# Four PSUM banks as one lasting tile, and attention's clips and exponentials on two banks at a time, in a two-layer cross-attention and feed-forward kernel

## The chip, the cores and the metric

The kernel runs on 1 core of one Trainium2 chip. The metric is device time in microseconds (us) of one execution. Engines are named as the profile names them: PE is TensorE's matmul pipe and PEld its weight loads, DVE is VectorE, ACT is ScalarE, POOL is GpSimd, SP issues most of the DMAs. PSUM is the memory that matmuls write; a tile of 128 partitions by 512 float32 values is called a bank here, and no matmul of this kernel writes across two.

## The reference

Eight batches of 112 tokens (512 wide) go through two layers, each a cross-attention and a feed-forward, with a layer norm in front of each and the result added to `x`. The context has 375 rows per batch.

```python
x = x + _L0_xattn_ref(_layernorm(x), ctx_2048, mask_bool)     # one head, keys and values are ctx itself
x = x + _L0_ffn_ref(_layernorm(x), w1, w2, w3)                # bit-linear: ternary weights, 8-bit activations
x = x + _L1_xattn_ref(_layernorm(x), ctx_2048, mask_int, Wq, bq, Wk, bk, Wv, bv, Wo, bo, ...)
x = x + _L1_ffn_ref(_layernorm(x), wq_gate, s_gate, wq_up, s_up, wq_down, s_down)
```

The change lies in the third line, and it touches the fourth through the PSUM banks. The third line's attention has 16 heads of 32:

```python
scores = einsum('bhsd,bhtd->bhst', q, k) / sqrt(32)
scores = clip(scores, -50, 50)
scores = clip(where(attend, scores, -10000.0), -50, 50)
probs  = softmax(scores)
ctx    = einsum('bhst,bhtd->bhsd', probs, v)
delta  = layernorm(clip(residual_scale, 0, 0.3) * (ctx @ Wo.T + bo)) * ln_gamma + ln_beta
```

The fourth line is `down(silu(gate(x)) * up(x))` with a hidden width of 1408 and integer weights minus 128, scaled per row.

## The kernel before

Line numbers are those of the kernel before, as the profile has them.

**Token layout.** The 8 x 112 tokens are 7 tiles of 128 (`tokens`, `xs`). Layer 1's matmuls over tokens go in two groups, tiles 0 to 3 (512 columns) and tiles 4 to 6 (384 columns) (`GROUPS`).

**Order.** PE's and SP's instructions run in the order in which the code writes them throughout. From layer 0's attention to its end, and in layer 1's attention, the order on DVE, ACT and POOL is also the written one; in the queries (L764 to L780) and in the last feed-forward those three engines are ordered by the scheduling layer. That layer also places every semaphore wait. It takes them from the tiles: a tile is what `pool.tile(...)` returns, an instruction that reads a tile waits for the one that wrote it, and one that writes it waits for those that read it before. A pool with `bufs=4` hands out four buffers in turn, and a new tile in a buffer waits until the old tile in the same buffer has been used up.

**PSUM from layer 1 on.** `ps_s` (L708) is a pool of four one-bank tiles, all called `s`; `ps_mm` (L709) has two, called `mm`; attention adds `num` and `den` (`ps_av`), and the last feed-forward adds two called `down` (`ps_d`).

**Who uses `ps_s`, in order:**

- `queries(g)` (L730 to L749): for each of four 128-row pieces `dc` of Wq, eight matmuls into an `mm` tile (L738, L740), then four into an `s` tile (L744); ACT moves `mm` to `qT` (L746), and DVE subtracts the `s` tile from it (L748). It runs for group 0, then for group 1.
- `transpose2(i)` (L222 to L236), for token tiles 4, 5 and 6 between the pieces of group 0's queries: four PE transposes into an `s` tile (L227), an ACT copy (L230), a DVE subtraction that reads the same `s` tile (L233), and a DVE operation on SBUF (L234).
- `scores(b, c)` (L899 to L912), for each of the 8 batches `b` and 3 context chunks `c` of 125: four `s` tiles, one for each 32-row strip `r` of the key and query projections; 16 matmuls of 32 x 125 weights and 112 columns (L905), with `dc` outside and `r` inside, so that four heads' scores fill each tile; then for each `r` a DVE clip from PSUM to an SBUF tile `e` (L910) and an ACT exponential in place (L911).
- `hits` (L992), one small matmul at attention's end, whose maximum decides between two ways of doing the last feed-forward; here the first, `feed_forward1`, is run.
- `gate_up1(g, ...)` (L1035 to L1055): for each of 11 pieces `hc` of the hidden width a gate tile and an up tile. It is called for pieces 0 and 1 of group 0, then `project(6)` runs, then for pieces 2 to 10, then after the down projections of group 0 for all 11 pieces of group 1.
- `transpose4` (L840) for token tiles 4, 5 and 6, between the down projections of group 0.

The core of `gate_up1`, one piece:

```python
gate = ps_s.tile([P, 512], F32, name="s")                                  # L1039
up = ps_s.tile([P, 512], F32, name="s")                                    # L1040
...                                                                        # 8 matmuls into gate, then 8 into up: L1045
nc.scalar.activation(gu, gate, AF.Silu, scale=sg)                          # L1050
nc.vector.scalar_tensor_tensor(gu, up, su, gu, ALU.mult, ALU.mult)         # L1051
nc.scalar.copy(gus[0], gu)                                                 # L1053
nc.vector.tensor_sub(gus[1], gu, gus[0])                                   # L1054
```

**Around the scores.** In each turn of attention's loop (L957 to L1002) PE also runs a step of the next batch's key and value projections (`fill`, L194 and L203), the sums of the chunk before (`sums`: L926 and L931) and, from batch 2 on, an output projection (L803) with its layer norm on DVE and POOL. `add(b)` (L893) adds the exponentials of chunk 1 to those of chunk 0, on POOL except for the last batch. `divide(b)` (L941) takes reciprocals (L947) and multiplies (L948) on DVE. `project_begin` and `project_end` (L806, L820) hold the layer norm's DVE and POOL operations (L809 to L828).

Of the kernel before, what the change touches and what calls it, by code (L numbers as in the profile page):

```python
# [23 lines left out]
F32 = mybir.dt.float32  # L24
# [6 lines left out]
ALU = mybir.AluOpType  # L31
AX = mybir.AxisListType
PSUM = bass.MemoryType.PSUM
ENGINES = mybir.EngineType

P = 128
B, T, D = 8, 112, 512
KC = D // P
S2, CK = 375, 125
NCK = S2 // CK  # L40
# [5 lines left out]
NR = P // HD  # L46
# [10 lines left out]
CLIP = 50.0 / SC1  # L57
# [7 lines left out]

SPLIT = 2.0 ** -12
LESS = 1.0 - 2.0 ** -13


@with_exitstack  # L70
def two_layers(ctx: ExitStack, tc: tile.TileContext, x, ctxT, ctxN, mask0, mask1, w1, w2, w3,
               wq, wk, wv, wo, bq, bk, bv, bo, gamma, beta, rscale,
               wg, sg, wu, su, wd, sd, out):
    nc = tc.nc
# [147 lines left out]
    def transpose2(i, psum):  # L222
# [6 lines left out]
        high, low, diff = (t[:, :, j * P:(j + 1) * P] for t in h2T[g])  # L229
        nc.scalar.activation(high, pt, AF.Identity, scale=LESS)  # L230

# [7 lines left out]
    with tc.tile_pool(name="w0", bufs=1, side="right") as w0p, \  # L239
# [290 lines left out]
        with tc.tile_pool(name="work1", bufs=2, side="right") as work1:  # L530
# [90 lines left out]
            for i in range(2, NT):  # L621
# [54 lines left out]
                elif i == 4:  # L676
# [3 lines left out]
                                                 for name in ("wq_high", "wq_low", "h2T_high"))  # L680
                    nc.scalar.activation(wq_high, wq_s, AF.Identity, scale=LESS)
                    nc.gpsimd.tensor_sub(wq_low, wq_s, wq_high.bitcast(F32))
# [22 lines left out]

    tailp = ctx.enter_context(tc.tile_pool(name="tailp", bufs=1, side="right"))

    ps_s = ctx.enter_context(tc.tile_pool(name="ps_s1", bufs=4, space=PSUM))  # L708
    ps_mm = ctx.enter_context(tc.tile_pool(name="ps_mm1", bufs=2, space=PSUM))  # L709
    kv_psum[0] = ps_mm  # L710

# [11 lines left out]
    upper = tailp.tile([CK, NCK, B], F32, name="upper")  # L723
# [127 lines left out]
    with tc.tile_pool(name="work2", bufs=1, side="right") as work2, \  # L851
# [21 lines left out]
        def convert_integers():  # L873
            for raw, which, half, c, n in loaded:
# [12 lines left out]

        sets = [[work2.tile([P, KC, T], F32, name=f"e{i}{r}") for r in range(NR)]  # L890
                for i in range(NCK)]

        def add(b):  # L893
            add = (nc.gpsimd if b in ADD_POOL else nc.vector).tensor_add
            for r in range(NR):
                e, e1 = (sets[(b + c) % NCK][r][:CK] for c in range(2))
                add(e, e, e1)  # L897

        def scores(b, c):  # L899
            kT = kvs_of[b][0]  # L900
            ss = [ps_s.tile([CK, KC, T], F32, name="s") for r in range(NR)]
            for dc in range(KC):
                for r in range(NR):
                    rows = slice(r * HD, (r + 1) * HD)
                    nc.tensor.matmul(ss[r][:, dc, :], lhsT=kT[rows, dc, c * CK:(c + 1) * CK],  # L905
                                     rhs=qT[rows, dc, b * T:(b + 1) * T], start=True, stop=True)
            es = sets[(b + c) % NCK]
            for r in range(NR):
                e = es[r][:CK]
                nc.vector.tensor_scalar(e, ss[r], upper[:, c, b:b + 1], -CLIP, ALU.min, ALU.max)  # L910
                nc.scalar.activation(e, e, AF.Exp, scale=SC1)  # L911
            return es  # L912

# [41 lines left out]
        for b in range(B):  # L957
            for c in range(NCK):
                if c == 2 and b in ADD_POOL:
                    add(b)  # L960
                if (b, c) in due:
                    convert_integers()
                    if counts:
                        load_integers(counts.pop(0))
                es = scores(b, c)
                if c == 2 and b not in ADD_POOL:
                    add(b)
# [237 lines left out]
```

## Time and profile before

| what | value |
|---|---|
| median of 3 runs | 517.08 us (516.91 to 518.55) |
| the profiled execution | 516.34 us, of which the span from the first to the last instruction is 514.2 us |
| granted PE clock, mean | 0.997 |
| queries, 213.20 to 235.30 us | PE busy 21.91 of 22.10 us |
| attention, 235.30 to 395.60 us | PE busy 158.84 of 160.30 us, DVE 124.70, ACT 98.28, POOL 83.48 |
| gate and up, group 0, with `project(6)`, 395.60 to 439.50 us | PE busy 43.90 of 43.90 us, DVE 25.70, ACT 13.90 |
| gate and up, group 1, 462.20 to 492.70 us | PE busy 30.50 of 30.50 us, DVE 13.15, ACT 11.55 |

How to read it: the busy time of an engine is the time covered by its instructions' rows. Matmuls overlap each other, and their ends are modelled, so PE's share near 100% says only that there is hardly a hole between matmuls. The profile's groups give, for one line and one shape, the count, the total busy time, the mean of one in ns, and how long the engine had stood idle in front of them and for whom. The chain of waits runs from the last instruction back to what released it, step by step.

### The profile page before, as it was taken

The page shows a single profiled execution, that of the slowest core. Times are in us where ns is not written, and L with a number is a line of the kernel's source. Part 1 is how long each engine was busy: PE and PEld are TensorE (multiplying, and loading weights), DVE is VectorE, ACT ScalarE, POOL GpSimd, SP SyncE. Part 2 cuts the span into 40 slices and gives each one's busy share as a digit, 9 for nine tenths or more (in the row PEclk, how much of TensorE's full clock was granted, in tenths as well). Part 3 has the DMA queues.
Part 4 walks back from the last instruction along what each step waited for, and adds up shares of the span by engine and source line. Part 5 has one row for each costly group of instructions (what it writes and reads, how often), then busy time and mean ns, then how long its engine had stood idle before and what let it go on. Part 6 is the DMA issues. An engine that isn't in the chain of part 4 may idle for free.

```text
span 514.2 us, 8868 instructions
## 1 busy us (share of the span) xinstructions
PE 502.5 (98%) x3402; PEld 315.8 (61%) x3402; DVE 337.2 (66%) x815; ACT 252.8 (49%) x438; POOL 134.4 (26%) x221
## 2 busy tenths in 40 slices
PE   9999999999999999999999999999999999999995
PEld 6445554455545455696565565555555788889984
DVE  3552548767798987965676688986897753334432
ACT  0326656857565666236675366465665233103310
POOL 0000121110111064211551475674754430000000
PEclk9999999999999999999999999999999999999998
DMA  8998795200120100122421112012320000010001
GB/s 241 347 407 326 268 324 205 80 18 0 61 82 1 60 2 0 45 101 61 162 68 51 62 52 62 3 53 62 98 69 13 20 1 1 20 42 20 1 20 48
DMA packets 13489, 45.77 MB, mean 89 GB/s; under 512 B 2097, under 2 KB 3392, under 8 KB 12288
## 3 DMA queue, kind: packets, MB, share of 16 engines
q1 hardware_dynamic: 11888, 41.43, 23.5%
q0 software_dynamic: 1248, 3.70, 2.2%
q8 instruction: 29, 0.48, 0.4%
q14 instruction: 20, 0.16, 0.1%
q10 hardware_dynamic: 304, 0.01, 0.0%
HBM read 41.46 MB, written 1.84 MB: 84 GB/s over the span
## 4 chain that ended last, share of the span: by engine, by line
PE 47%; DVE 6%; POOL 2%; ACT 1%; DMA 1%; issue 1%; DVEq 0%; POOLq 0%; ACTq 0%
PE s L1045 14%; PE mm L203 8%; PE down L1067 7%; PE mm L803 3%; PE s L905 3%; PE num L931 2%; PE mm L194 2%; DVE e L910 2%; PE den L926 2%; PE mm L740 1%; PE mm L738 1%; DMA raw<-in_wd_dram 1%; PE s L744 1%; DVE e L947 1%; ACT e L911 1%
## 5 line engine op out<-in xcount | busy, mean ns | idle before, releaser
L203 PE MATMUL mm<-wv,cT 128*125 128x512 f32 x192 | 87.6, 599 | 0.0
L194 PE MATMUL mm<-cT,wk 128*128 128x375 f32 x256 | 87.3, 485 | 0.0
L1045 PE MATMUL s<-h4T,w 128*128 128x512 f32 (+1 forms) x352 | 72.6, 367 | 0.2 <-PE num L931 0.2
L1045 PEld LDWEIGHTS s<-h4T,w 128*128 128x128 f32 x352 | 63.5, 188 | 8.8 <-PE num L931 0.4
L910 DVE TENSOR_SCALAR e<-s,upper 125x448 f32<-125x448 f32 x96 | 59.0, 677 | 14.7 <-PE s L905 13.9
L911 ACT ACTIVATE e<-e 125x448 f32<-125x448 f32 x96 | 51.6, 570 | 27.8 <-DVE e L910 27.3
L194 PEld LDWEIGHTS mm<-cT,wk 128*128 128x128 f32 x256 | 46.8, 190 | 27.6 <-issue 1.0
L203 PEld LDWEIGHTS mm<-wv,cT 128*125 128x125 f32 x192 | 34.5, 187 | 38.0 <-issue 36.4
L897 POOL TENSOR_TENSOR e<-e,e 125x448 f32<-125x448 f32 x28 | 33.1, 1213 | 15.8 <-PE num L931 15.8
L1067 PE MATMUL down<-w,gu 128*128 128x512 f32 (+1 forms) x176 | 37.0, 367 | 0.0
L541 PE MATMUL mm<-w_q,q_qT 128*128 128x512 fp8e4 (+1 forms) x168 | 34.8, 361 | 0.8 <-DVE tokens L583 0.4
L439 POOL DMA_DIRECT2D tokens<-x x14 | 10.7, 768 | 90.3 <-DVE x L433 63.0
L1067 PEld LDWEIGHTS down<-w,gu 128*128 128x128 f32 x176 | 29.8, 188 | 5.7
L880 ACT ACTIVATE w<-raw,zero_point 128x640 fp32r<-128x640 int32 (+2 forms) x29 | 22.6, 781 | 20.4 <-DMA raw<-in_wd_dram 9.2
L1053 ACT CAST gu<-gu 128x512 fp32r<-128x512 f32 (+1 forms) x22 | 12.5, 568 | 39.6 <-DVE gu L1051 39.6
L570 POOL TENSOR_SCALAR q<-gu 128x704 bf16<-128x704 f32 x14 | 10.8, 790 | 79.8 <-ACT gu L567 79.8
L882 POOL TENSOR_SCALAR w<-raw 128x640 fp32r<-128x640 int32 (+2 forms) x29 | 20.7, 724 | 36.0 <-ACT w L880 35.8
L905 PE MATMUL s<-qT,kv 32*125 32x112 f32 x768 | 29.4, 280 | 0.6 <-DVE qT L748 0.3
L1051 DVE SCALAR_TENSOR_TENSOR gu<-s,su,gu 128x512 f32<-128x512 f32 (+1 forms) x22 | 15.1, 684 | 21.8 <-PE s L1045 20.6
L905 PEld LDWEIGHTS s<-qT,kv 32*125 32x125 f32 x768 | 24.5, 183 | 7.1 <-issue 5.8
L541 PEld LDWEIGHTS <-q_qT 128*128 128x128 bf16 x168 | 16.3, 98 | 19.7 <-issue 2.5
L931 PEld LDWEIGHTS num<-e,kv 125*32 125x32 f32 x768 | 18.4, 110 | 13.6 <-issue 7.9
(238 smaller groups left out, 798.6 us busy)
## 6 DMA issues: line engine op xcount, KB each, us to landing
cT<-in_ctxT_dram SPq DMA_DIRECT2D x13, 750.0 KB, 6.1
raw<-in_w_dram SPq DMA_DIRECT2D x6, 1408.0 KB, 20.3
cN<-in_ctxN_dram SPq DMA_DIRECT2D x8, 768.0 KB, 4.5
raw<-in_wg_dram SPq DMA_DIRECT2D x8, 320.0 KB, 3.0
raw<-in_wu_dram SPq DMA_DIRECT2D x8, 320.0 KB, 2.9
raw<-in_wd_dram SPq DMA_DIRECT2D x8, 320.0 KB, 3.1
out_dram<-d SPq DMA_DIRECT2D x6, 256.0 KB, 2.0
wk<-in_wk_dram SPq DMA_DIRECT2D x4, 256.0 KB, 4.9
```

What stands on the lines that cost most here:

```text
L194: nc.tensor.matmul(ps[dc], lhsT=wk_s[:, kc, dc * P:(dc + 1) * P], rhs=cT[:, kc, :], start=(kc == 0), stop=(kc == KC - 1))
L203: nc.tensor.matmul(ps, lhsT=cT[:, kc, c * CK:(c + 1) * CK], rhs=wv_s[:, kc, :], start=(kc == 0), stop=(kc == KC - 1))
L541: nc.tensor.matmul(ps[:, :n], lhsT=qT[:, kc, :], rhs=w[:, kc * H + n0:kc * H + n0 + n], start=(kc == 0), stop=(kc == KC - 1))
L880: nc.scalar.activation(t, raw, AF.Square, bias=zero_point, accum_out=squares[:, k:k + 1])
L882: nc.gpsimd.tensor_scalar(t, raw, -128.0, 1.0, ALU.add, ALU.mult)
L897: add(e, e, e1)
L905: nc.tensor.matmul(ss[r][:, dc, :], lhsT=kT[rows, dc, c * CK:(c + 1) * CK], rhs=qT[rows, dc, b * T:(b + 1) * T], start=True, stop=True)
L910: nc.vector.tensor_scalar(e, ss[r], upper[:, c, b:b + 1], -CLIP, ALU.min, ALU.max)
L911: nc.scalar.activation(e, e, AF.Exp, scale=SC1)
L931: nc.tensor.matmul(num[r * HD:(r + 1) * HD, dc, :], lhsT=v[:, c, head], rhs=es[r][:CK, dc, :], start=(c == 0 and dc == 0), stop=(c == NCK ...
L1045: nc.tensor.matmul(ps[:, :n], lhsT=w[:, c:c + P], rhs=h4T[k][:, kc, :n], start=(kc == 0 and k == 0), stop=(kc == KC - 1 and k == 1))
L1067: nc.tensor.matmul(ps, lhsT=gus[k][:, hc, j * P:(j + 1) * P], rhs=w[:, c + n0:c + n0 + n], start=(hc == 0 and k == 0), stop=(hc == HC - 1 ...
```

## The change

The four one-bank tiles become one tile of four banks, allocated once from a pool with one buffer and used from the queries to the end. A small class hands out parts of it: `tile` gives the next bank, `pair` the next two neighbouring banks that begin at an even one. In `scores`, two strips share a pair of banks and an `e` tile of twice the width, and one clip and one exponential take both: 48 clips and 48 exponentials of 896 columns in place of 96 and 96 of 448. `add` takes the double tiles too: 16 additions in place of 32. The matmuls, their number, their shapes and their order on PE stay as they were, and so does every DMA. The other users of `ps_s` keep their code and get one bank at a time from `tile`.

```diff
+class Banks:
+    def __init__(self, pool):
+        self.all = pool.tile([P, 4, 512], F32, name="s")
+        self.next = 0
+
+    def tile(self, shape, dtype, name):
+        n = 1
+        for d in shape[1:]:
+            n *= d
+        t = self.all[:shape[0], self.next, :n]
+        self.next = (self.next + 1) % 4
+        return t if len(shape) == 2 else t.rearrange("p (a b) -> p a b", a=shape[1])
+
+    def pair(self):
+        k = (self.next + 1) // 2 * 2 % 4
+        self.next = (k + 2) % 4
+        return self.all[:, k:k + 2, :]
...
-    ps_s = ctx.enter_context(tc.tile_pool(name="ps_s1", bufs=4, space=PSUM))
+    ps_s = Banks(ctx.enter_context(tc.tile_pool(name="ps_s1", bufs=1, space=PSUM)))
...
-        sets = [[work2.tile([P, KC, T], F32, name=f"e{i}{r}") for r in range(NR)]
+        twos = [[work2.tile([P, 2, KC, T], F32, name=f"e{i}{h}") for h in range(NR // 2)]
                 for i in range(NCK)]
+        sets = [[two[r // 2][:, r % 2] for r in range(NR)] for two in twos]
 
         def add(b):
             add = (nc.gpsimd if b in ADD_POOL else nc.vector).tensor_add
-            for r in range(NR):
-                e, e1 = (sets[(b + c) % NCK][r][:CK] for c in range(2))
+            for h in range(NR // 2):
+                e, e1 = (twos[(b + c) % NCK][h][:CK] for c in range(2))
                 add(e, e, e1)
 
         def scores(b, c):
             kT = kvs_of[b][0]
-            ss = [ps_s.tile([CK, KC, T], F32, name="s") for r in range(NR)]
+            ss = [ps_s.pair() for h in range(NR // 2)]
             for dc in range(KC):
                 for r in range(NR):
                     rows = slice(r * HD, (r + 1) * HD)
-                    nc.tensor.matmul(ss[r][:, dc, :], lhsT=kT[rows, dc, c * CK:(c + 1) * CK],
+                    nc.tensor.matmul(ss[r // 2][:CK, r % 2, dc * T:(dc + 1) * T], lhsT=kT[rows, dc, c * CK:(c + 1) * CK],
                                      rhs=qT[rows, dc, b * T:(b + 1) * T], start=True, stop=True)
-            es = sets[(b + c) % NCK]
-            for r in range(NR):
-                e = es[r][:CK]
-                nc.vector.tensor_scalar(e, ss[r], upper[:, c, b:b + 1], -CLIP, ALU.min, ALU.max)
+            for h in range(NR // 2):
+                e = twos[(b + c) % NCK][h][:CK].rearrange("p a k t -> p a (k t)")
+                nc.vector.tensor_scalar(e, ss[h][:CK, :, :KC * T], upper[:, c, b:b + 1], -CLIP,
+                                        ALU.min, ALU.max)
                 nc.scalar.activation(e, e, AF.Exp, scale=SC1)
-            return es
+            return sets[(b + c) % NCK]
```

## The prediction

> **What bounds the kernel now.** I read the page from the top, then the chain of waits, then the groups by form, then single stretches of the timeline.
>
> ```profile
> span 514.2 us, 8868 instructions
> PE 502.5 (98%) x3402; PEld 315.8 (61%) x3402; DVE 337.2 (66%) x815; ACT 252.8 (49%) x438; POOL 134.4 (26%) x221
> ...
> PE   9999999999999999999999999999999999999995
> ...
> PE s L1045 14%; PE mm L203 8%; PE down L1067 7%; PE mm L803 3%; PE s L905 3%; PE num L931 2%; PE mm L194 2%; DVE e L910 2%; PE den L926 2%; PE mm L740 1%; PE mm L738 1%; DMA raw<-in_wd_dram 1%; PE s L744 1%; DVE e L947 1%; ACT e L911 1%
> ...
> L910 DVE TENSOR_SCALAR e<-s,upper 125x448 f32<-125x448 f32 x96 | 59.0, 677 | 14.7 <-PE s L905 13.9
> L911 ACT ACTIVATE e<-e 125x448 f32<-125x448 f32 x96 | 51.6, 570 | 27.8 <-DVE e L910 27.3
> ```
>
> PE has no hole in any slice. DVE and ACT are a half to two thirds busy, and the clips and exponentials mostly stand idle in front of themselves, waiting for PE. So work saved on DVE or ACT is worth only what PE waits for it, and a new PE wait costs its full length. The heaviest entry of the chain is L1045, the gate and up matmuls, which use the same `s` banks as the scores. Their stretches, their consumers, and how fast waits pass:
>
> ```profile
> 406.75:440.34 33.59, 33.59 (x144) 26.70 (x143) 1.00 0.00 1
> 462.16:492.69 30.53, 30.53 (x176) 30.21 (x175) 1.00 0.03 9
> ...
> L1051 DVE SCALAR_TENSOR_TENSOR gu<-s,su,gu 128x512 f32<-128x512 f32 x11 | 8.3, 751 | 10.2 <-PE s L1045 9.0 <-DMA sd<-in_sd_dram 1.2
> L1050 ACT ACTIVATE gu<-s,sg 128x512 f32<-128x512 f32 x11 | 7.6, 687 | 8.3 <-DVE qT L948 4.6 <-PE s L1045 3.6
> L1051 DVE SCALAR_TENSOR_TENSOR gu<-s,su,gu 128x384 f32<-128x384 f32 x11 | 6.8, 618 | 11.6 <-PE s L1045 11.6
> L1050 ACT ACTIVATE gu<-s,sg 128x384 f32<-128x384 f32 x11 | 6.4, 583 | 8.1 <-PE s L1045 8.1
> ...
> 213.49 0.58 PE L738 MATMUL mm<-h2T_high,wq_high 128*128 128x512 f32 x1
> 213.91 0.39 PE L740 MATMUL mm<-h2T,wq_low 128*128 128x512 f32 x1
> ...
> 219.52 0.69 DVE L748 TENSOR_TENSOR qT<-qT,s 128x512 f32<-128x512 f32 x1 [0.63 <-PE s L744]
> 265.37 2.46 DVE L910 TENSOR_SCALAR e<-s,upper 125x448 f32<-125x448 f32 x4
> 267.88 0.19 PEld L905 LDWEIGHTS s<-qT,kv 32*125 32x125 f32 x3 [0.30 <-DVE e L910]
> 403.87 0.75 DVE L1051 SCALAR_TENSOR_TENSOR gu<-s,su,gu 128x512 f32<-128x512 f32 x1 [1.24 <-DMA sd<-in_sd_dram]
> 422.91 0.63 PE L1045 MATMUL s<-h4T,w 128*128 128x512 f32 x2
> 423.64 0.69 ACT L1050 ACTIVATE gu<-s,sg 128x512 f32<-128x512 f32 x1 [0.45 <-PE s L1045]
> ```
>
> The first two lines are stretches holding nothing but L1045 matmuls: PE busy throughout, 33.59 / 144 = 0.233 us a matmul in group 0 and 30.53 / 176 = 0.174 in group 1. So a step of `gate_up1` (16 matmuls) takes 3.73 or 2.78 us, and Silu (L1050) and product (L1051), 1.44 or 1.20 us together, run wholly beside the next step's matmuls. From the timeline rows: ACT starts 0.10 us after the matmul it waits for ends (422.91 + 0.63 = 423.54, then 423.64); PE's weight load starts 0.05 us after the DVE instruction it waits for (265.37 + 2.46 = 267.83, then 267.88); and the first matmul after a wait carries its weight load openly (L738: 0.58 in place of 0.39, 0.19 more).
>
> **The change part by part.** *Fewer, wider clips, exponentials and additions.* No row shows 896 columns. The slope comes from rows of two widths: L1051 (751 - 618) / 128 = 1.04 ns a column on DVE, L1050 (687 - 583) / 128 = 0.81 on ACT. A wide clip is 677 + 448 x 1.04 = 1143 ns, a wide exponential 570 + 364 = 934. DVE saves 48 x (1354 - 1143) = 10.1 us, ACT 48 x (1140 - 934) = 9.9, POOL a few on 14 additions of 1.2 us replaced. All lies beside PE, except where PE waits for a clip. PE's L905 blocks last 1.14 us in the timeline, except one of 1.95 (at 267.05) and one of 1.80 (at 300.70): 0.81 + 0.66 us. A few tenths more stand at two transposes (L844) and at the start of the scores: about 2.0 in all, the bound on the gain. Two groups of four clips precede the end of the first wait, each 0.18 us shorter (2.46 to 2.28), one the second's: 0.36 + 0.18, so I take 0.6. The bound from below is 0: the last exponential of a chunk ends 0.1 later than now (2.28 + 0.93 against 2.46 + 0.57), but its readers (L926, L931) stand behind 2.7 to 3.7 us of projection matmuls.
>
> *Four tiles become one.* This part decides. The scheduling layer derives waits tile by tile. In the changed program as built (instructions and semaphore counts, no times), a writer of any bank of `s` waits for the last reader of whichever bank was used before, and a reader for the last matmul into the tile. For `gate_up1`: now a gate matmul waits for the Silu two steps back; in the changed program it waits for the product L1051 of the step just before, and that step's Silu waits for its last *up* matmul, not its last gate matmul. The rotation through the banks is still there, the overlap is not. Behind the waiting weight load stands all of PE's queue. The bubble at each step, from the start of the last up matmul: matmul and wake 0.395 + 0.10, Silu 0.687, wake 0.06 (Silu's end 405.86 to L1051 at 405.92), L1051 0.751, wake 0.05, open weight load 0.19, minus the pitch that passes anyway 0.233: 2.00 us. In group 1: 0.336 + 0.10 + 0.583 + 0.06 + 0.618 + 0.05 + 0.19 - 0.174 = 1.76 us.
>
> How often: group 0 has ten step changes. Into step 1: L1051 of step 0 starts at 403.87 today, since DVE must first finish `divide(7)` and `project_end(5)`; step 1 starts at 395.60 + 3.73 = 399.33. It will start at 403.87 + 0.75 + 0.24 = 404.86: 5.53 us. Into step 2: `project(6)`, 3.43 us on PE, hides it. Into step 3: in the changed order DVE has L822 of `project(6)` ahead of the product of step 2 (today behind it). L809 to L822 takes 407.96 to 413.98 today, 6.02 us. On today's time scale step 2 ends at 404.86 + 3.73 + 3.43 + 3.73 = 415.75, L809 starts at 412.28, and 412.28 + 6.02 + 0.74 + 0.75 + 0.24 = 420.03: 4.28 us. Seven plain ones: 14.0. Group 1: ten, 17.6. Sum 41.4 us. The down projections lose nothing: their first 20 matmuls (20 x 0.233 = 4.7 us) need steps 0 to 9 only, and the last step's chain to L1054 takes 3.4.
>
> *The queries.* The transposes of token tiles 4 and 6 now wait for L748 of the piece before: 219.52 + 0.69 + 0.24 = 220.45 against 219.25 today, 1.20 us each. Tile 5's wait for tile 4's L233 (last transpose to L230 0.30, L230 0.60, 0.05, L233 0.68, 0.24, minus 0.11): 1.76 us. Sum 4.2. The L744 groups wait too, but behind eight matmuls (1.87 us in group 0, 1.39 in group 1), and need 1.24 to 1.68 and 1.05: hidden. In attention, the first score matmul now waits for the last clip of the chunk before, as the fourth did already: nothing.
>
> Sum against the profiled execution: 516.34 + 41.4 + 4.2 - 0.6 = 561.3. The median of the runs is 0.74 above that execution, so 562.
>
> A rule speaks against this sum. The Trainium skill, page "Perfetto Trace Analysis", section "Matmuls", says to rotate independent matmul groups through different PSUM banks so that evacuation of one overlaps the next group's matmuls. The changed kernel still rotates, and by the rule alone it would stay at about 516; what the rule leaves out is that the waits must also be per bank.
>
> Matmuls can also run at half pace: the first ones (L462, 128 columns) start 0.21 us apart, the like transposes at 219.25 0.11 apart, though the granted clock reads 1.00 in both. No row shows whether bubbles of 2 us bring it back; the 0.99 us hole before 206.94 does not. The bounds are nothing, and every one of the 17 bubbled steps at half speed: 7 x 3.73 + 10 x 2.78 = 54 us. I take nothing, nearest the one hole seen. The skill's page "TensorE: Matmul & The Clock Gate", section "Why this matters for your kernels", puts the limit at idle gaps of about 3 us; by it only the bubbles of 5.5 and 4.3 would cost, at most 1.7 us each, and the sum would be some 565.
>
> **The rivals.** *Per-bank waits after all* (not slower): if I read the built counts wrongly and they are met two steps back as today, L1050 and L1051 stay beside the matmuls and only the 0.6 us counts: 515.7 in the profile, 516.5 as a median. It decides once the plain bubbles are under 0.03 us each (0.6 / 17), with no 1.2 us ones in the queries. For it: 100% PE share in those stretches today. Against: the built waits. Were the chain's 1.8% of L910 all PE's loss, it would be 9 us faster; PE's full rows speak against that.
>
> *Half the overlap stays*: Silu runs beside the up matmuls and only L1051 is exposed. Steps cost 1.25 and 1.12 us: 7 x 1.25 + 10 x 1.12 = 20.0 in place of 31.6, so 550. Against it: Silu's built wait names the last up matmul.
>
> *The bubbles slow the matmuls too*: half of the bound of 54 us gives 562 + 27 = 589.
>
> **How the numbers follow.** The forecast 0.87, half overlap 0.05, slowed matmuls 0.04, per-bank waits 0.04 (half of it above, half below the limit of 0.3%, about what a measurement of this kernel can tell from no change). 0.25 us more or less in each of 17 plain bubbles is 4; the two long ones and the queries may be off by 2 each: 553 to 571. Chances: faster 0.02, same 0.02, slower 0.96.
>
> **What would show it.** Right: PEld of L1045 idle for L1051, near 2.0 and 1.8 us a step; group 0's gate and up stretch near 68 us from 43.9, group 1's near 48 from 30.5; L910 48 times at 1.14 us; transposes L227 idle for L748 and L233. Wrong: L1045's pitch unbroken, or bubbles that vary with DVE's other work. A start-to-start of 0.47 us between L1045 matmuls would show the half pace.

## The result, and the profile after

| | before | after |
|---|---|---|
| median | 517.0 us (4 runs, 516.2 to 518.55) | 565.41 us (4 runs, 565.10 to 566.82) |
| ratio | | 1.0938, 95% interval 1.0906 to 1.0969 |
| the profiled execution, its span | 516.34, 514.2 us | 565.26, 563.4 us |
| start of the queries | 213.49 | 213.95 |
| queries | 21.13 | 25.70 (+4.6) |
| attention | 160.97 | 161.81 (+0.8) |
| gate and up, group 0, with `project(6)` | 44.58 | 71.96 (+27.4) |
| down, group 0 | 21.82 | 21.82 |
| gate and up, group 1, first to last matmul | 30.35 | 46.86 (+16.5) |
| from there to the end | 21.89 | 21.27 (-0.6) |

Each stage lasts from the start of its first matmul to that of the next stage's, so a wait in front of a stage's first matmul counts to the stage before. Lines of the kernel after are those of before plus 22 to 24: L1069 is the gate and up matmul (L1045), L1074 Silu, L1075 the product, L933 the clip, L935 the exponential, L249 the queries' transposes, L770 the queries' subtraction, L866 attention's transposes, L921 `add`, L972 `divide`'s multiplication.

The page of the kernel after, its head and the groups that answer to those shown before:

```profile
span 563.4 us, 8695 instructions
PE 511.7 (91%) x3402; PEld 316.9 (56%) x3402; DVE 335.1 (59%) x765; ACT 247.0 (44%) x390; POOL 130.1 (23%) x207
...
PE   9999999999999998999999989989786768986696
...
PEclk9999999999999999999999999999977999999999
...
L1069 PE MATMUL s<-h4T,w 128*128 128x512 f32 (+1 forms) x352 | 82.5, 389 | 34.1 <-DVE gu L1075 33.9
...
L933 DVE TENSOR_SCALAR e<-s,upper 125x896 f32<-125x896 f32 x48 | 53.0, 1145 | 16.5 <-PE s L929 15.6
...
L935 ACT ACTIVATE e<-e 125x896 f32<-125x896 f32 x48 | 44.9, 947 | 36.1 <-DVE e L933 34.1
...
L1074 ACT ACTIVATE gu<-s,sg 128x512 f32<-128x512 f32 (+1 forms) x22 | 13.9, 634 | 79.8 <-PE s L1069 75.1
```

The holes are in PE's last quarter. L1069 stood idle 34 us for L1075, and L1074 stood idle 75 us for L1069: PE, ACT and DVE take turns instead of working side by side. The clips did fall from 59.0 to 53.0 us of DVE and the exponentials from 51.6 to 44.9 of ACT, and their idle times grew. One plain step of group 0 in the timeline:

```profile
441.48 4.00 PE L1069 MATMUL s<-h4T,w 128*128 128x512 f32 x16 [1.62 <-DVE gu L1075]
...
445.58 0.69 ACT L1074 ACTIVATE gu<-s,sg 128x512 f32<-128x512 f32 x1 [3.50 <-PE s L1069]
446.30 0.75 DVE L1075 SCALAR_TENSOR_TENSOR gu<-s,su,gu 128x512 f32<-128x512 f32 x1 [3.50 <-ACT gu L1074]
...
447.10 1.20 PE L1069 MATMUL s<-h4T,w 128*128 128x512 f32 x4 [1.62 <-DVE gu L1075]
```

Matmuls end at 445.48, Silu starts 0.10 later, the product 0.03 after Silu, the next step 0.05 after the product. A step takes 447.10 - 441.48 = 5.62 us; 16 matmuls without a hole take 3.73 (33.59 us for 144, before). So a plain bubble costs 1.89 us; in group 1 the period is 4.435, 16 matmuls take 2.78, and the bubble is 1.66.

The two long holes cost more than their length. Windows of the kernel after (length; busy time of PE, PEld, DVE, ACT, POOL; granted clock; DMA's share and GB/s):

```profile
405.73:409.14 3.41, 0.00 (x0) 0.00 (x0) 2.65 (x7) 0.69 (x1) 0.70 (x3) 1.00 0.30 72
409.14:412.55 3.41, 2.02 (x5) 1.64 (x6) 1.44 (x2) 0.62 (x1) 2.52 (x6) 0.50 0.03 10
412.55:415.97 3.42, 3.42 (x10) 2.64 (x9) 0.00 (x0) 0.00 (x0) 0.43 (x1) 0.50 0.00 0
...
439.85:443.27 3.42, 1.80 (x9) 1.48 (x9) 1.44 (x2) 1.31 (x2) 0.00 (x0) 1.00 0.00 0
```

Step 1 starts at 410.53 under a clock of 0.50, its matmuls start 0.427 us apart and it lasts 6.45 us in place of 3.99. Step 3 does the same, 6.30. Together they lose 4.8 us. The last window holds a plain bubble and keeps the clock at 1.00.

In the queries the three transposes wait as foreseen, 0.85 + 1.41 + 0.85 us of idle PE:

```profile
220.72 0.66 PE L249 MATMUL s<-ident,d 128*128 128x128 f32 x4 [0.85 <-DVE qT L770]
222.78 0.66 PE L249 MATMUL s<-ident,d 128*128 128x128 f32 x4 [1.41 <-DVE h2T L255]
...
227.08 0.66 PE L249 MATMUL s<-ident,d 128*128 128x128 f32 x4 [0.85 <-DVE qT L770]
```

Part of the queries' +4.6 is no new time. The first scores wait for the queries' last subtraction in both kernels, but at different places in the block. First the kernel before, then the kernel after:

```profile
234.63 0.48 PE L905 MATMUL s<-qT,kv 32*125 32x112 f32 x6
235.41 1.12 PE L905 MATMUL s<-qT,kv 32*125 32x112 f32 x26 [0.31 <-DVE qT L748]
```

```profile
239.66 1.14 PE L929 MATMUL s<-qT,kv 32*125 32x112 f32 x32 [0.72 <-DVE qT L770]
```

Before, it falls behind the block's sixth matmul and the block takes 1.91 us; after, it falls ahead of the first one and the block takes 1.14. So 0.77 us has moved across the border between the two stages. Put back, the queries cost 3.8 us more and attention 1.6.

Attention hides two movements under its +0.8. Counted from the first score matmul, the 13th score block (batch 4, chunk 0) starts 1.98 us *earlier* than before. Of this, 0.77 is the wait that moved; the other 1.2 is what the wider clips and exponentials gave PE. Then two transposes give it all back and more, 1.6 us before batch 5's first block and 1.2 before batch 7's. PE's waits in attention, kernel after (total, times, longest):

```profile
PE mm L866 <- ACT kv L219: 1.6, 1, 1.6
PE mm L866 <- DVE d L859: 1.4, 1, 1.4
```

What made DVE late there is `divide`'s multiplication beside `add` on POOL. First the kernel before, then the kernel after, each from its timeline:

```profile
322.69 0.36 DVE L948 TENSOR_TENSOR qT<-qT,e 128x192 f32<-128x192 f32 x1
322.78 1.27 POOL L897 TENSOR_TENSOR e<-e,e 125x448 f32<-125x448 f32 x1 [1.30 <-PE num L931]
```

```profile
325.84 2.08 POOL L921 TENSOR_TENSOR e<-e,e 125x896 f32<-125x896 f32 x1 [0.71 <-PE num L955]
326.10 2.04 DVE L972 TENSOR_TENSOR qT<-qT,e 128x192 f32<-128x192 f32 x1
```

The same multiplication takes 0.36 us where it starts ahead of the addition and 2.04 where it starts behind: it ends 0.22 us after the addition. All eight multiplications that overlap an addition in the kernel after end behind the end of the one in progress, by 0.15 us (128 columns), 0.21 and 0.22 (192), 0.29 (256), 0.35 twice (320), 0.42 (384) and 0.49 (448), about 1.1 ns a column: as if each began when the addition ended. The Trainium skill, page "SBUF — State Buffer", section "🔬 SBUF: two separate sides", says that VectorE and GpSimd share one pair of ports as an exclusive lock for a whole instruction, and that a VectorE operation with two SBUF inputs takes part in it; these rows agree. An addition of twice the width can hold them up for 2.08 us in place of 1.14, the time of one addition.

### The profile page after: what moved, and what is told of

Read it like the earlier page. It is cut to its first block, busy times and chain, and to the rows that moved or that the text cites. A ratio compares the mean times of both kernels' runs of the same rounds, so it can differ in the third digit from the quotient of the medians.

```text
span 563.4 us, 8695 instructions
## 1 busy us (share of the span) xinstructions
PE 511.7 (91%) x3402; PEld 316.9 (56%) x3402; DVE 335.1 (59%) x765; ACT 247.0 (44%) x390; POOL 130.1 (23%) x207
## 4 chain that ended last, share of the span: by engine, by line
PE 43%; DVE 13%; POOL 2%; ACT 2%; issue 1%; DMA 1%; DVEq 0%; ACTq 0%; POOLq 0%; SPq 0%
PE s L1069 13%; PE mm L225 7%; PE down L1091 6%; PE mm L825 3%; PE s L929 3%; DVE e L933 3%; DVE gu L1075 2%; DVE e L971 2%; PE num L955 2%; PE mm L216 2%; ACT gu L1074 2%; DVE qT L972 1%; PE den L950 1%; PE mm L762 1%; PE mm L760 1%
## 5 line engine op out<-in xcount | busy, mean ns | idle before, releaser
L1069 PE MATMUL s<-h4T,w 128*128 128x512 f32 (+1 forms) x352 | 82.5, 389 | 34.1 <-DVE gu L1075 33.9
L1069 PEld LDWEIGHTS s<-h4T,w 128*128 128x128 f32 x352 | 66.0, 198 | 50.2 <-DVE gu L1075 41.1
L933 DVE TENSOR_SCALAR e<-s,upper 125x896 f32<-125x896 f32 x48 | 53.0, 1145 | 16.5 <-PE s L929 15.6
L935 ACT ACTIVATE e<-e 125x896 f32<-125x896 f32 x48 | 44.9, 947 | 36.1 <-DVE e L933 34.1
L1075 DVE SCALAR_TENSOR_TENSOR gu<-s,su,gu 128x512 f32<-128x512 f32 (+1 forms) x22 | 15.0, 684 | 65.6 <-ACT gu L1074 64.4
L1074 ACT ACTIVATE gu<-s,sg 128x512 f32<-128x512 f32 (+1 forms) x22 | 13.9, 634 | 79.8 <-PE s L1069 75.1
L921 POOL TENSOR_TENSOR e<-e,e 125x896 f32<-125x896 f32 x14 | 30.7, 2217 | 14.9 <-PE num L955 13.1
L1091 PEld LDWEIGHTS down<-w,gu 128*128 128x128 f32 x176 | 29.8, 188 | 5.7
L929 PE MATMUL s<-qT,kv 32*125 32x112 f32 x768 | 27.4, 279 | 1.5 <-DVE e L933 0.8
L929 PEld LDWEIGHTS s<-qT,kv 32*125 32x125 f32 x768 | 23.1, 183 | 7.7 <-issue 4.7
L825 PE MATMUL mm<-wo,qT 128*128 128x512 f32 x56 | 25.8, 603 | 0.5 <-DVE qT L972 0.5
```

Source lines behind the costliest of these rows:

```text
L825: nc.tensor.matmul(ps, lhsT=qT[:, kc, i * P:(i + 1) * P], rhs=wo_s[:, kc, :], start=(kc == 0), stop=(kc == KC - 1))
L929: nc.tensor.matmul(ss[r // 2][:CK, r % 2, dc * T:(dc + 1) * T], lhsT=kT[rows, dc, c * CK:(c + 1) * CK], rhs=qT[rows, dc, b * T:(b + 1) * T ...
L933: nc.vector.tensor_scalar(e, ss[h][:CK, :, :KC * T], upper[:, c, b:b + 1], -CLIP, ALU.min, ALU.max)
L1069: nc.tensor.matmul(ps[:, :n], lhsT=w[:, c:c + P], rhs=h4T[k][:, kc, :n], start=(kc == 0 and k == 0), stop=(kc == KC - 1 and k == 1))
L1074: nc.scalar.activation(gu[:, :n], gate[:, :n], AF.Silu, scale=sg_s[:, hc:hc + 1])
L1075: nc.vector.scalar_tensor_tensor(gu[:, :n], up[:, :n], su_s[:, hc:hc + 1], gu[:, :n], ALU.mult, ALU.mult)
```

## The experiments

**The lasting tile without the pairs.** Clips, exponentials and additions as in the kernel before, the four banks still one tile:

```diff
-            ss = [ps_s.pair() for h in range(NR // 2)]
+            ss = [ps_s.tile([CK, KC, T], F32, name="s") for r in range(NR)]
...
-                nc.vector.tensor_scalar(e, ss[h][:CK, :, :KC * T], upper[:, c, b:b + 1], -CLIP,
-                                        ALU.min, ALU.max)
+                nc.vector.tensor_scalar(e, ss[r], upper[:, c, b:b + 1], -CLIP, ALU.min, ALU.max)
```

> The lasting four-bank tile alone; clips, exponentials and additions one strip at a time as before. If the tile costs the time (waits tile by tile): the queries near 25.7 us and everything from the first gate matmul on near 162 us, as in the changed kernel, attention within 2 us of 161, the whole 562 to 568 us. If the double-width instructions cost it: 517 us, the plain gate and up steps back at 3.77 and 2.78 us.

Measured: 563.9 us in one run, beside 516.62 for the kernel before. Attention took 160.71, everything from the first gate matmul on 160.3. PE's waits:

```profile
PE s L1068 <- DVE gu L1074: 33.9, 19, 5.0
```

The same 33.9 us in the same 19 waits as in the kernel after (there 33.9, 19, 5.1). From the first gate matmul on the tile alone costs the time; the wide instructions' share is the 1.1 us by which the changed kernel's attention is longer (161.81). The 160.3 lies 1.6 under the kernel after's 161.9, because each of the two long holes was followed by one stretch of 3.41 us at a clock of 0.50 here and by two there. Attention here confirms the moved wait: with the old clips it is 0.76 us ahead after the first block, and still only 0.73 at the 13th. The queries took 27.26, 1.6 more than expected, since one stretch of 3.41 us there ran at a granted clock of 0.50.

**Two lasting tiles of two banks.** Same banks, same order, same widths:

```diff
-        self.all = pool.tile([P, 4, 512], F32, name="s")
+        self.both = [pool.tile([P, 2, 512], F32, name=f"s{k}") for k in range(2)]
...
-        t = self.all[:shape[0], self.next, :n]
+        t = self.both[self.next // 2][:shape[0], self.next % 2, :n]
...
-        return self.all[:, k:k + 2, :]
+        return self.both[k // 2]
```

> The same banks as two lasting tiles of two banks, handed out in the same order. One small tile more is taken at attention's end, so in group 0 a step's up tile shares its lasting tile with the next step's gate tile, and in group 1 gate and up of one step share one. If a wait goes by the tile: in group 1 a step's matmuls wait for the product two steps back, all hidden, 2.78 us a step and 30.7 us in all (47.2 in the changed kernel); in group 0 the next gate matmul still waits for the product of the step before, but Silu no longer waits for the up matmuls, so a plain bubble is the product alone, 1.1 to 1.25 us in place of 1.85; the queries back at 21.3 us; the whole near 540. If a lasting tile as such costs the time, or if the banks' neighbourhood does: both groups as in the changed kernel, 565.

Measured: 537.83 us, one run. Group 0's and group 1's gate and up matmuls alone (windows: length, PE busy, PEld busy, clock, DMA), then a plain step of group 0 in the timeline:

```profile
400.90:461.93 61.03, 45.69 (x176) 33.36 (x176) 0.97 0.01 5
483.59:514.28 30.69, 30.69 (x176) 30.36 (x175) 1.00 0.02 9
```

```profile
443.21 3.99 PE L1069 MATMUL s<-h4T,w 128*128 128x512 f32 x16 [0.91 <-DVE gu L1075]
...
445.43 0.69 ACT L1074 ACTIVATE gu<-s,sg 128x512 f32<-128x512 f32 x1 [1.62 <-PE s L1069]
447.31 0.75 DVE L1075 SCALAR_TENSOR_TENSOR gu<-s,su,gu 128x512 f32<-128x512 f32 x1 [2.77 <-PE s L1069]
...
448.12 1.20 PE L1069 MATMUL s<-h4T,w 128*128 128x512 f32 x4 [0.91 <-DVE gu L1075]
```

In one kernel, with the same matmuls and the same four lasting banks: where gate and up of a step share a tile, no bubble at all; where a step's up shares one with the next step's gate, Silu starts beside the up matmuls (445.43) and only the product is exposed, 448.12 - 443.21 = 4.91 a step, a bubble of 1.18. So in the feed-forward neither lasting tiles nor neighbouring banks cost anything of themselves. What shares a tile decides. My figure for the queries (21.3) was wrong, 23.91 measured: there the second transpose shares its tile with the first and the third with a piece's L770, and these two still wait (1.5 and 0.9 us in PE's waits), while the first no longer does.

**Filling the long holes.** The kernel after, with idle matmuls of group 0's shape into a spare `mm` bank after steps 0 and 2, 12 and 8 of them, then 8 and 4:

```diff
+                for k in range({0: 12, 2: 8}.get(hc, 0) if g == 0 else 0):
+                    if k == 0:
+                        idle = ps_mm.tile([P, D], F32, name="mm")
+                    nc.tensor.matmul(idle, lhsT=w[:, c:c + P], rhs=h4T[0][:, 0, :],
+                                     start=True, stop=True)
                 gu = work3.tile([P, 512], F32, name="gu")
```

> The changed kernel with idle work in front of two long PE holes: 12 matmuls of 512 columns into a spare mm bank after step 0 and 8 after step 2, so that the holes before steps 1 and 3 shrink from 5.07 and 3.79 us to about 2.2 and 1.9 while these steps start when they did. If a hole of that length is what slows the matmuls behind it: start to start 0.235 us from the first matmuls on, both steps near 4.0 us in place of 6.45 and 6.30, the whole 4.8 us shorter, 560.5. If something else in these stretches slows them (DVE, POOL or the DMA running beside): still 0.43 us start to start, 565.3.

> As the run before, with 8 and 4 idle matmuls: holes of about 3.2 us before step 1 and 2.85 before step 3. This places the length at which a hole slows the matmuls: the holes of 3.79 us and more did, those of 1.6 did not. If it lies above 3.2: both steps near 4.0 us, 560.5. If it lies between 2.85 and 3.2: step 1 near 6.4 and step 3 near 4.0, 563. If below 2.85: both near 6.3, 565.3. The Trainium skill, page "TensorE: Matmul & The Clock Gate", section "Why this matters for your kernels", speaks of idle gaps of about 3 us, which would make it the second.

Measured: 563.61 and 564.53 us, one run each. Steps 1 and 3 in the timeline, with 12 and 8 and then with 8 and 4:

```profile
411.87 4.00 PE L1069 MATMUL s<-h4T,w 128*128 128x512 f32 x16 [2.32 <-DVE gu L1080]
...
426.84 5.54 PE L1069 MATMUL s<-h4T,w 128*128 128x512 f32 x16 [1.95 <-DVE gu L1080]
```

```profile
411.80 6.54 PE L1069 MATMUL s<-h4T,w 128*128 128x512 f32 x16 [3.23 <-DVE gu L1080]
...
429.29 4.00 PE L1069 MATMUL s<-h4T,w 128*128 128x512 f32 x16 [2.86 <-DVE gu L1080]
```

The second run taken alone would put a limit between 2.9 and 3.2 us. The first forbids any limit by length: a hole of 2.32 us does nothing and one of 1.95 slows the matmuls. And it slows them late, after four of step 3 at the full pace. The windows of that run show why:

```profile
424.51:427.92 3.41, 1.47 (x7) 0.90 (x6) 2.52 (x5) 0.62 (x1) 0.62 (x3) 1.00 0.00 0
427.92:431.33 3.41, 3.41 (x10) 2.67 (x9) 0.63 (x4) 0.00 (x0) 2.03 (x7) 0.50 0.00 0
```

The clock changes only at the edges of a grid of 3.413 us. The hole of 1.95 lies in one window whole, PE is busy 1.47 of 3.41 us in it (43%), and the *next* window gets half the clock. The hole of 2.32 us before step 1 is cut by an edge (410.85), 62% and 70% are left, and nothing happens. So the theory (holes slow the matmuls) holds against its rival, since filling them without touching DVE, POOL or DMA freed one step in each run; its measure (the length of the hole) falls. The whole fell by 1.7 and 0.7 us only, because step 3 or step 1 stayed slow and a window of the queries ran at 0.50 in both runs.

**Pairs only where they are used.** `ps_s` is closed before attention, which takes two-bank tiles in turn from a pool of two; the last feed-forward opens four one-bank tiles again. Once with additions one strip wide, once with the changed kernel's:

```diff
-    ps_s = Banks(ctx.enter_context(tc.tile_pool(name="ps_s1", bufs=1, space=PSUM)))
     ps_mm = ctx.enter_context(tc.tile_pool(name="ps_mm1", bufs=2, space=PSUM))
+    banks = ExitStack()
+    ps_s = banks.enter_context(tc.tile_pool(name="ps_s1", bufs=4, space=PSUM))
...
+    banks.close()
     with tc.tile_pool(name="work2", bufs=1, side="right") as work2, \
+            tc.tile_pool(name="ps_p", bufs=2, space=PSUM) as ps_p, \
...
-            ss = [ps_s.pair() for h in range(NR // 2)]
+            ss = [ps_p.tile([P, 2, 512], F32, name="s") for h in range(NR // 2)]
...
+            tc.tile_pool(name="ps_s2", bufs=4, space=PSUM) as ps_s, \
```

> Pairs only where they are used: attention takes two-bank tiles in turn from a pool of two, the queries and the last feed-forward four one-bank tiles as before; clips and exponentials two strips wide, the additions one strip wide (448 columns). If the whole loss was the one tile, and attention's 2.0 us of gains in the changed kernel were given back by divide's multiplications standing behind the double-width additions on POOL: queries 21.3, attention about 159, the rest 118.6 us, 515.0 in all, 0.996 of the time before. If the double-width clips and exponentials themselves made attention later: attention near 161.8, 517.9 in all.

> As the run before, but with the changed kernel's 16 additions of 896 columns. If divide's multiplications wait for the addition that POOL is in: two or three of them take 1.2 to 2.0 us in place of 0.3 to 0.8, transposes of the layer norm's tokens wait for DVE and ACT, attention near 161.8 us as in the changed kernel, 517.9 in all, 1.002 of the time before. If the width of the additions does not matter: the same as the run before, 515.0.

Measured, in five rounds: 517.14 us with one-strip additions (before 516.39; ratio 1.0009, interval 1.0000 to 1.0018) and 519.22 with wide ones (1.0049, 1.0035 to 1.0063). In both, both groups of the feed-forward are back at 44.56 and 30.35 us. Attention takes 160.40 and 161.87. The multiplication of 192 columns, with one-strip and then with wide additions:

```profile
323.43 4.71 POOL L902 TENSOR_TENSOR e<-e,e 125x448 f32<-125x448 f32 x4 [0.65 <-PE num L936]
323.74 1.04 DVE L953 TENSOR_TENSOR qT<-qT,e 128x192 f32<-128x192 f32 x1
```

```profile
322.95 4.23 POOL L902 TENSOR_TENSOR e<-e,e 125x896 f32<-125x896 f32 x2 [0.71 <-PE num L936]
323.22 2.02 DVE L953 TENSOR_TENSOR qT<-qT,e 128x192 f32<-128x192 f32 x1
```

It waits for one addition of 1.14 us or of 2.08; over the whole of attention the multiplications cost DVE 9.4 us with narrow additions and 13.6 with wide ones (10.6 in the kernel before, 13.5 after). The width of the additions is therefore worth 161.87 - 160.40 = 1.5 us of PE's time. My theory that the additions alone gave attention's gain back was only half right: with narrow ones attention is 0.6 us shorter and not 2.0, and even this is the wait that moved, since here too the first score matmul waits 0.7 us for L749. Queries and attention together take 182.24 us, and 182.10 in the kernel before: nothing is gained. Attention is 1.87 ahead at the 13th block, 0.77 of it by that wait, and two transposes take 0.8 and 0.45 back (PE's waits: 1.2 us for DVE, 0.8 for ACT). The pools cost a little too: the first `mm` matmul stands 0.9 us at the swap. The queries start at 215.31 and 214.84, against 213.49 before; what the swap leaves unexplained of that lies in layer 0, whose code neither version changes, and the cause stays open.

**Can the gain be kept?** The version with narrow additions, `mm` on PSUM's other side, and the DVE operation that writes the transposes' tokens issued ahead of the clips; and that last edit (`write4`) on the kernel before:

```diff
-    ps_mm = ctx.enter_context(tc.tile_pool(name="ps_mm1", bufs=2, space=PSUM))
+    ps_mm = ctx.enter_context(tc.tile_pool(name="ps_mm1", bufs=2, space=PSUM, side="right"))
...
+                if c == 2 and 3 <= b < 3 + GROUPS[0][1]:
+                    write4(b - 3)
                 es = scores(b, c)
...
-                    if turned:
-                        write4(b - 3)
```

> The version with two-bank pool tiles and one-strip additions, with two repairs: mm lies in the other half of PSUM, where its first matmul does not wait for layer 0's last readers (0.9 us there), and the DVE operation that writes the tokens for the transposes in attention is issued ahead of the chunk's clips instead of behind them, since the transposes waited 1.2 us for it. If those are what kept attention from its gain of 2.0 us: queries start near 213.5, attention 159.0 to 159.7, the whole 515.0 to 515.6, a ratio of 0.997 to 0.9985. If DVE's chain as a whole is what PE meets there: attention stays near 160.4 and the whole at 516.2, a ratio of 0.9995.

> The kernel before with the second of these repairs alone, one-bank tiles and one-strip clips. Its transposes wait 0.4 and 0.3 us for ACT, not for that DVE operation, so if the gain of the run above comes from the wider clips this stays at 516.4 plus or minus 0.5, a ratio of 0.999 to 1.001; if the repair is worth the time by itself it takes what the run above takes.

Measured, in five rounds beside 516.80: 516.64 us (ratio 0.9994, interval 0.9985 to 1.0004) and 517.71 (1.0029, 1.0016 to 1.0043). PE's waits in the first:

```profile
PE mm L845 <- ACT kv L197: 1.8, 2, 1.0
```

The wait for DVE is gone and a wait for ACT has grown in its place: the transposes' bank is one that a key projection used, its copy on ACT stands behind the exponentials, and those stand behind clips that now start one operation later. Attention stays at 160.44. On the kernel before the same edit costs 1.3 us of attention, which neither of the two expectations allowed for; PE's waits for that copy are 2.1 us there. By these waits DVE and ACT together are what PE meets, and none of these versions is measurably faster than the kernel before.

## Why the prediction was right, point by point

The direction, the place and the mechanism held: 562 predicted, 565.41 measured. Against the profiled execution the sum was 561.3 and the measurement 565.26. The miss of 3.9 us is what is left of larger ones that partly cancel. Term by term:

- *Plain bubbles.* Predicted 2.00 and 1.76 us, measured 1.89 and 1.66; 17 of them came to 29.8 in place of 31.6. The open weight load was sized from one row (0.19): here the first pitch of a step is 0.337 against 0.235, so it costs 0.10, and the wake from ACT to DVE is 0.03, not 0.06.
- *The two long holes.* Predicted 5.53 and 4.28, the steps start 5.33 (410.53 - 401.47 - 3.73) and some 4.0 us late. The reason that I gave for the first was incomplete: DVE was done with `project_end(5)` at 408.55, and until the product at 409.72 it loads the flag that chooses the feed-forward's variant (0.55 us), branches and passes five semaphore waits. The row that I showed names a DMA for that idle time. That DMA landed at 409.77, after the product had begun, so the product did not wait for it.
- *Matmuls at half pace.* This is the term that was mis-sized. I took nothing, by the one hole that I had seen (0.99 us on the weight load's row, 0.82 on the matmul's), with bounds of 0 and 54. It is 4.8 us, 2.46 and 2.30 in the two steps behind the long holes, and that is more than the whole miss. The Trainium skill's rule that was weighed against it (page "TensorE: Matmul & The Clock Gate", section "Why this matters for your kernels") named the right two steps, and the sum by it was 565. That was in part luck: it took at most 1.7 us for each, and the experiments show that the length of a hole is not what decides. The 1.00 that I read beside the slow first matmuls was no reading either: the clock's records in that trace begin at 5.49 us.
- *The queries.* 4.2 predicted, 4.57 measured; 3.8 of it stands at the three transposes named, 0.8 is the wait in front of the first score matmul, for which I had said "nothing" and which the kernel before has inside its first block.
- *Attention.* -0.6 predicted, +0.84 measured, or +1.6 with the moved wait put back. The clip and the exponential came at 1145 and 947 ns (1143 and 934 predicted), and the gain on PE by the 13th block was 1.2, twice what I took. My list of long score blocks lacked the 21st (1.48 us) and counted the first (1.91) among "a few tenths". What failed is the sentence that put the wide additions down as some POOL time saved: I did not ask what DVE does while POOL adds, and the last link, that readers of late exponentials are hidden, left out the transposes.
- *The down projections lose nothing*: 21.82 in both.
- The rivals fell as priced against: the waits are not per bank, and the half overlap (plain bubbles of 1.25) was seen only where two lasting tiles gave it, at 1.18. Slowed matmuls came, but behind two holes, not behind seventeen.

By stages the miss of 3.9 us is: half pace +4.8, bubbles and holes -2.3, queries +0.4, attention +1.4 (with the moved wait put back -0.4 and +2.2), the tail -0.6, and +0.3 from layer 0 and what lies outside the span, which this change does not touch.

## What to carry to other kernels

Where a scheduling layer takes its waits from tiles, the tile is the unit of overlap: merge buffers into one only if all of them are consumed together and another tile is left to write into meanwhile, and check for every other user which instruction it now waits for. Widening an addition on POOL from 1.14 to 2.08 us lengthened the waits of the DVE multiplications behind it and cost PE 1.5 us, so a saving in instruction count may be paid elsewhere. Price a hole on PE by how much of a clock window it empties, not by its length alone.

## What the runs showed of the hardware that was not expected

The granted clock moves on a fixed grid of 3.413 us and follows how busy PE was in the window before. Over all ten profiles (some 1500 windows): at full clock every window with PE busy 52% or more was followed by full clock, and every one with 43% or less (0 to 43%, twelve windows, two of them at the end of a run) by half. At half clock, windows with 49, 59 and 65% were followed by half, those with 94% or more by full. Between 43 and 52%, and on the way up between 65 and 94%, nothing was seen. The Trainium skill, page "TensorE: Matmul & The Clock Gate", section "What's actually happening", gives the same free-running window of 3413 ns; it speaks of an idle window as what brings the low clock, and here a window that was 43% busy did.

So the same hole is free or costs up to two windows at half pace, by where the grid falls: the queries ran at full clock in the kernel after's profile and lost a window in three of the experiments' (27.26 us against 25.70), with the same waits.
